# Reordering the setup of layer 0 in a four-layer graph network: first loads, degrees and weights

## The chip, the cores and the metric

The kernel runs on one core of one Trainium2 chip. Its time is the device time of one execution in microseconds; the median of several executions is given. The profile is of one further execution.

## What is computed

64 graphs of 256 nodes pass through four layers, each of the form "layer norm of x plus the layer's output". Layer 0 is a recurrence over the nodes; it is the only one that the change touches:

```
d         = sum(adj, axis=-1)                                # degree of each node
dinv      = where(d != 0, 1/d, 0)
norm_adjT = swapaxes(adj, 1, 2) * dinv[:, :, None]

def step(h, i):                                              # i = 0 .. 255, one after the other
    x     = h_e[:, i]
    x_par = einsum('bj,bjd->bd', norm_adjT[:, i], h)         # h: already updated up to i-1
    iou   = x @ W_ioux.T + b_ioux + x_par @ W_iouh.T + b_iouh
    r, z  = sigmoid(split(iou, 2))
    hc    = tanh(x @ W_coux.T + b_coux + (x_par * r) @ W_couh.T + b_couh)
    h[:, i] = z * x_par + (1 - z) * hc
```

Layers 1 to 3 (a graph convolution, a masked attention, an attention with 8 heads) come after it and are not changed.

## The kernel before

`_recurrence` computes layer 0. All 64 graphs go through a step together. Node i needs a sum over all nodes j of adj[j, i] times the state of j. For j not yet updated (j at or above i) that state is x itself, so this part is known from the start: it is the x side. The kernel computes the x side for columns i = 0 to 127 ahead of the steps, and that for columns 128 to 255 in gaps of the steps.

Four things happen ahead of step 0.

1. Setup (lines 124 to 164). `_load_wT` loads the four weight matrices on SP's queue (L48), transposes them on PE into PSUM (L52) and copies them to `WxT` and `WhT` on DVE (L53). Six bias loads go out on ACT's queue (L133, L137). DVE adds them and cuts the sum in three bf16 parts (`_split_bf16`, L60 to L67), each stored by SP into `bias3` (L68). POOL makes the identity `ident`, a pattern `span`, which SP copies to `window` in eight small DMAs (L153), zeroes `Hw` (L158) and makes the triangular mask `tri` (L161).

2. The x side for columns 0 to 127 (lines 185 to 209), in eight groups of GB = 8 graphs. A group loads two halves of adj (`xA`, 512 KB each, SP, L193) and of x (`xX`, 1 MB each, ACT, L194), POOL masks one half with `tri` (L195), PE makes two products for each graph, one for each half of the rows j (L172), ACT and DVE by turns copy PSUM to `xu` (L208), and SP stores it to `Us` in HBM (`x_out`, L179). Tiles have two buffers, so a group's loads wait for the products of the group before the last.

3. Tables of block 0 (the first 32 nodes). `degrees(0)` (lines 267 to 293) loads adj's rows in four parts of 4 rows into one buffer, `rows` (L276), and reduces each (L279), so that a part is loaded after the one before it is reduced; then it inverts the degrees, and four DMAs store them to `dinv` (L293). `load_S(0)` loads the 32 x 32 piece `S` of adj for each graph, in runs of 32 numbers, and doubles it over the partitions (L527, L534). `chain_S`, `late_load`, `sums_in` (`ACC` from `Us`, L298) and `load_x` (`xq`, L554) fill what step 0 and the steps after it read.

4. The start of step 0: `flip_x` transposes `xq` (L563), `x_part` and `bias_part` begin the gates in PSUM (L582, L573), `xp` is `ACC` times `dinv` (L685), and the step flips it (L597), multiplies by `WhT` (L590) and takes the Sigmoid (L779). In step 0, `flip_x` of the next eight nodes stands on PE ahead of that product and reads `xq_1`.

The pools for the x side are closed before those of the tables and the steps (`blk`, `stream`, `work`, `ps`) are opened, and the latter take their place in SBUF and PSUM. Up to the first step the tile framework chooses the order of the instructions on each engine and derives the waits. From `tc.manual_schedule()` (line 708) on, each engine runs in the order of the source. Each engine runs its own stream in order; SP and ACT also issue DMAs, and an engine stands still while it waits to issue one.

Of the kernel before, what the change touches and what calls it, by code (L numbers as in the profile page):

```python
# [9 lines left out]
F32 = mybir.dt.float32  # L10
BF16 = mybir.dt.bfloat16
AF = mybir.ActivationFunctionType
ALU = mybir.AluOpType
AX = mybir.AxisListType
# [5 lines left out]
P = 128  # L20
# [50 lines left out]
def _recurrence(tc, ident, Hd, x, adj, W_ioux, b_ioux, W_iouh, b_iouh, W_coux, b_coux, W_couh, b_couh):  # L71
# [22 lines left out]
    U = 8  # L94
# [8 lines left out]
    with ExitStack() as ctx:  # L103
# [13 lines left out]
        def ring(lo, hi):  # L117

            while lo < hi:
                end = min(hi, (lo // W + 1) * W)  # L120
                yield lo, end, lo % W
                lo = end

        with tc.tile_pool(name="r_setup", bufs=1) as tmp, tc.tile_pool(
            name="r_setup_ps", bufs=2, space=bass.MemoryType.PSUM
        ) as tps:
            for WT, wi, wc, s in ((WxT, W_ioux, W_coux, "x"), (WhT, W_iouh, W_couh, "h")):
                _load_wT(nc, tmp, tps, wi, ident, lambda c: WT[:, :, c % 2, c // 2 * 2, :], "i" + s)
                _load_wT(nc, tmp, tps, wc, ident, lambda c: WT[:, :, c, 1, :], "c" + s)
            bx, bh = (tmp.tile([1, 2, 3, P], F32, name=f"bias_{s}") for s in "xh")  # L130
            for t, bi, bc in ((bx, b_ioux, b_coux), (bh, b_iouh, b_couh)):
                for g in range(2):
                    nc.scalar.dma_start(  # L133
                        t[:, :, 2 * g, :],
                        bi[g * D:(g + 1) * D].rearrange("(c d) -> c d", c=2).unsqueeze(0),
                    )
                nc.scalar.dma_start(t[:, :, 1, :], bc.rearrange("(c d) -> c d", c=2).unsqueeze(0))  # L137
            nc.vector.tensor_add(bx, bx, bh)
            _split_bf16(nc, tmp, bias3, bx, "bias")

            span = tmp.tile([W, T // U, U], F32, name="span")
            nc.gpsimd.memset(span, 1.0)
            nc.gpsimd.affine_select(
                out=span, in_=span, pattern=[[U, T // U], [0, U]], compare_op=ALU.is_ge,
                fill=0.0, base=W - T // 2 - LAG - 1, channel_multiplier=-1,
            )
            for w in range(2):
                first = (w * T - W + T // 2) % W  # L150
                for lo, hi, at in ring(first, first + W):
                    for g in range(2):
                        nc.sync.dma_start(  # L153
                            window[w][g * W + at:g * W + at + hi - lo],
                            span[lo - first:hi - first].rearrange("p a u -> p (a u)"),
                        )
        nc.vector.memset(ones3, 1.0)
        nc.gpsimd.memset(Hw, 0.0)  # L158

# [16 lines left out]
        def x_out(half, b, ub):  # L176

            for c in range(2):
# [2 lines left out]
                    ub[:, :, c * P:(c + 1) * P],  # L181
                )


        with tc.tile_pool(name="r_first", bufs=2) as tmp, tc.tile_pool(
            name="r_first_ps", bufs=4, space=bass.MemoryType.PSUM
        ) as tps:
            for g in range(0, B, GB):
                A = tmp.tile([P, 2, GB, P], F32, tag="A", name=f"xA_{g}")
                Xs = tmp.tile([P, 2, GB, D], F32, tag="X", name=f"xX_{g}")  # L190
                for jc in range(2):
                    rows = slice(jc * P, (jc + 1) * P)
                    nc.sync.dma_start(A[:, jc], adj[g:g + GB, rows, 0:P].rearrange("b j i -> j b i"))  # L193
                    nc.scalar.dma_start(Xs[:, jc], x[g:g + GB, rows, :].rearrange("b j d -> j b d"))  # L194
                nc.gpsimd.tensor_mul(  # L195
                    A[:, 0], A[:, 0], tri.unsqueeze(1).to_broadcast([P, GB, P])
                )
                for n in range(0, GB, 4):
                    ub = tmp.tile([P, 4, D], F32, tag="ub", name=f"xu_{g}_{n}")
                    for e in range(0, 4, 2):  # L200
                        pb = tps.tile([P, 2, D], F32, tag="x", name=f"xp_{g}_{n}_{e}")
                        for q in range(2):
                            b = n + e + q
                            x_product(
                                pb, q, [A[:, jc, b, :] for jc in range(2)],
                                [Xs[:, jc, b, :] for jc in range(2)],
                            )
                        (nc.vector.tensor_copy if e else nc.scalar.copy)(ub[:, e:e + 2, :], pb)  # L208
                    x_out(0, g + n, ub)

        blk = ctx.enter_context(tc.tile_pool(name="r_blk", bufs=2))
        stream = ctx.enter_context(tc.tile_pool(name="r_stream", bufs=2))
        work = ctx.enter_context(tc.tile_pool(name="r_work", bufs=2))
        ps = ctx.enter_context(tc.tile_pool(name="r_ps", bufs=1, space=bass.MemoryType.PSUM))


        now = 0
# [49 lines left out]
        def degrees(k):  # L267

            R = 4
            HT = T // 2  # L270
            deg = work.tile([P, HT], F32, tag="deg", name=f"deg_{k}")
            for r in range(0, HT, R):
                rows = stream.tile([P, R, N], F32, tag="rows", name=f"rows_{k}_{r}", bufs=1)
                for h in range(2):
                    at = k * T + h * HT + r
                    nc.sync.dma_start(rows[h * B:(h + 1) * B], adj[:, at:at + R, :])  # L276
                yield
                for e in range(0, R, 2):
                    nc.vector.tensor_reduce(  # L279
                        deg[:, r + e:r + e + 2], rows[:, e:e + 2, :], AX.X, ALU.add  # L280
                    )
                    yield
            zero = work.tile([P, HT], F32, tag="deg0", name=f"deg0_{k}")
            nc.vector.tensor_scalar(zero, deg, 0.0, None, ALU.is_equal)
            nc.vector.tensor_add(deg, deg, zero)
            nc.vector.reciprocal(deg, deg)
            nc.vector.tensor_scalar(zero, zero, -1.0, 1.0, ALU.mult, ALU.add)
            nc.vector.tensor_mul(deg, deg, zero)
            yield
            for h in range(2):  # L290
                at = k * T + h * HT
                for c in range(2):
                    nc.sync.dma_start(dinv[c * B:(c + 1) * B, at:at + HT], deg[h * B:(h + 1) * B])  # L293

        def sums_in(a):

# [360 lines left out]
        pushes = []  # L657
        ring_in = []

        for _ in degrees(0):  # L660
            pass
        tables[0]["S"], double = load_S(0)
        double()
        tables[0]["Sd"] = chain_S(0)
        tables[0]["An"] = late_load(0)
        for a in range(3):
            sums_in(a)

        xq = {0: load_x(0)}
        for e in range(2):  # L670
            flip_x(0, e, xq[0])
            next_of(copies, 0)
        xq[1] = load_x(1)
        rc = ps.tile([P, 2, P], F32, tag="rc", name="rc_0", bufs=2)
        z = ps.tile([P, P], F32, tag="z", name="z_ps_0")
        for G, gates in ((rc, slice(0, 2)), (z, 2)):
# [695 lines left out]
```

## Time and profile before

| | |
|---|---|
| median of 3 runs | 3609.26 us (3601.38 to 3611.15) |
| profiled execution | 3613.04 us, span 3611.1 us |
| granted TensorE clock, mean | 0.975 |
| busy: PE, DVE, ACT, POOL | 91%, 66%, 53%, 41% of the span |
| from the span's start to the first load of the x side | 21.09 us |
| last store of the x side issued / landed | 120.93 / 123.45 us |
| `dinv` in place, first Sigmoid of step 0 | 151.9, 158.32 us |

Times in the profile count from the start of the span. A line such as `41.00 10.37 DMA Us<-xu` in the chain of waits says that from 41.00 us on, for 10.37 us, what ended last was waiting for that transfer. In busy time by stretch, each engine has its busy time in that stretch and the number of its instructions in brackets; "PEld" is the loading of PE's stationary operand, and the last three columns are the granted clock, the busy share of the DMA engines and what they moved.

### The profile page before, as it was taken

How to read it: one execution, taken by the hardware profiler on the slowest of the kernel's cores; microseconds unless marked ns; L12 is line 12 of the kernel's file. 1: busy time of each engine (PE TensorE's matmuls, PEld its weight loads, DVE VectorE, ACT ScalarE, POOL GpSimd, SP SyncE). 2: the span in 40 equal slices, each digit the busy share in tenths (PEclk: the TensorE clock that was granted, in tenths of full speed). 3: DMA queues.
4: the chain of work that ended last, by engine and by line, in shares of the span. 5: the costliest groups of instructions: out<-in, count | busy, mean ns of one | idle time of the engine just before them, and what ended most of it. 6: DMA issues, size and time to landing. Idle time of an engine off the chain costs nothing.

```text
span 3611.1 us, 81391 instructions
## 1 busy us (share of the span) xinstructions
PE 3296.8 (91%) x30374; PEld 2341.3 (65%) x30374; DVE 2375.3 (66%) x7052; ACT 1904.6 (53%) x5026; POOL 1485.1 (41%) x1669
## 2 busy tenths in 40 slices
PE   5599989999889898858999999999999999999998
PEld 4355555555555555536777777777777777777776
DVE  2366767776667777735676666677776667777775
ACT  0145545554445454425666666666666666666664
POOL 2266667766566778722222222222222222222221
PEclk9799999999999999978999999999999999999999
DMA  8746666788876564140111111111111111111100
GB/s 284 215 134 145 157 167 151 165 191 204 193 190 156 156 152 115 57 114 18 45 45 45 45 45 45 45 45 45 45 45 45 45 45 45 45 44 42 45 27 22
DMA packets 389636, 348.48 MB, mean 97 GB/s; under 512 B 107244, under 2 KB 355192, under 8 KB 384120
## 3 DMA queue, kind: packets, MB, share of 16 engines
q1 hardware_dynamic: 367280, 323.84, 33.7%
q10 hardware_dynamic: 21960, 19.41, 1.6%
q8 instruction: 242, 3.96, 0.5%
q14 instruction: 154, 1.26, 0.1%
HBM read 224.01 MB, written 99.61 MB: 90 GB/s over the span
## 4 chain that ended last, share of the span: by engine, by line
PE 71%; DVE 7%; DMA 7%; POOL 5%; issue 4%; ACT 4%; SPq 2%; ACTq 0%; DVEq 0%; POOLq 0%
PE mm L948 13%; PE o L1151 7%; PE rc L590 4%; PE s L1131 4%; PE rc L582 3%; PE mm_2f L948 3%; PE mm_3v L948 3%; PE mm_3f L948 3%; PE mm_g L948 3%; PE mm_t L948 3%; PE mm_2s L948 3%; PE mm_2v L948 3%; PE mm_2w L948 3%; DVE ACC L615 3%; PE tr_x L938 3%
## 5 line engine op out<-in xcount | busy, mean ns | idle before, releaser
L615 DVE SCALAR_TENSOR_TENSOR ACC<-keep,S,ACC 128x128 f32<-128x128 f32 x1712 | 504.1, 344 | 191.9 <-ACT hs L633 175.6
L917 POOL TENSOR_TENSOR rstd<-rstd,mhalf 128x2 f32<-128x2 f32 x256 | 172.9, 693 | 627.9 <-DVE rstd L916 626.2
L651 POOL TENSOR_TENSOR ACC<-ACC,far 128x384 f32<-128x384 f32 (+1 forms) x313 | 371.5, 1187 | 24.6
L1138 DVE TENSOR_TENSOR p<-s,neg 128x512 f32<-128x512 f32 x512 | 317.4, 681 | 69.0 <-PE s L1131 69.0
L582 PE MATMUL rc<-WxT,xqT 128*64 128x256 f32 x2048 | 328.9, 400 | 7.5 <-issue 2.5
L925 ACT ACTIVATE y<-y,shift,rstd 128x256 f32<-128x256 f32 x512 | 273.4, 598 | 92.4 <-DVE shift L923 53.0
L1043 POOL TENSOR_TENSOR y<-y,g 128x512 f32<-128x512 f32 x64 | 80.8, 1262 | 567.7 <-issue 556.8
L647 POOL TENSOR_TENSOR far<-hs,S 128x384 f32<-128x384 f32 (+1 forms) x313 | 304.2, 972 | 4.7
L1139 ACT ACTIVATE p<-p 128x512 f32<-128x512 f32 x512 | 294.8, 626 | 2.6 <-DVE p L1138 1.6
L913 DVE BATCH_NORM_STATS2 st<-y 128x6 f32<-128x256 f32 x512 | 208.9, 408 | 94.6 <-POOL y L1043 89.8
L755 POOL TENSOR_TENSOR ready<-ACC,dinv 128x128 f32<-128x128 f32 x255 | 101.9, 399 | 399.3 <-DVE ACC L615 380.2
L1166 DVE TENSOR_TENSOR y<-y,mm_3f 128x512 f32<-128x512 f32 x64 | 44.0, 687 | 281.3 <-PE mm_3f L948 281.3
L1157 DVE RECIPROCAL rT<-o 128x256 f32<-128x256 f32 x128 | 224.0, 1750 | 0.3 <-PE o L1151 0.3
L1054 ACT ACTIVATE qk<-mm,b_cols 128x256 f32<-128x256 f32 x256 | 107.2, 469 | 203.7 <-PE mm L948 203.7
L1029 ACT COPY xT<-tr_x 128x512 f32<-128x512 f32 x192 | 112.3, 586 | 183.0 <-PE tr_x L938 183.0
L599 ACT COPY xpT<-xpT_ps 128x128 f32<-128x128 f32 x256 | 68.1, 266 | 263.7 <-PE xpT_ps L597 263.7
L590 PE MATMUL rc<-WhT,xpT 128*64 128x128 f32 x2048 | 170.4, 288 | 28.7 <-ACT xpT L599 28.5
L590 PEld LDWEIGHTS rc<-WhT,xpT 128*64 128x64 f32 x2048 | 107.8, 137 | 118.5 <-ACT xpT L599 83.8
L948 PE MATMUL mm<-xT,W2q 128*128 128x256 f32 x512 | 129.4, 396 | 44.6 <-ACT xT L1029 44.6
L582 PE MATMUL z_ps<-WxT,xqT 128*64 128x128 f32 x2048 | 169.8, 287 | 0.0
L1106 ACT ACTIVATE qk<-mm,b_cols 128x256 f32<-128x256 f32 x256 | 107.2, 469 | 118.5 <-PE mm L948 118.5
L1008 POOL TENSOR_TENSOR dis<-dis,mhalf 128x2 f32<-128x2 f32 x64 | 44.1, 689 | 292.0 <-DVE dis L1007 292.0
(167 smaller groups left out, 7988.8 us busy)
## 6 DMA issues: line engine op xcount, KB each, us to landing
xX<-in_x_dram ACTq DMA_DIRECT2D x16, 1024.0 KB
Us<-xu SPq DMA_DIRECT2D x64, 256.0 KB
rows<-in_adj_dram SPq DMA_DIRECT2D x64, 256.0 KB
ACC<-Us SPq DMA_DIRECT2D x32, 512.0 KB
xq<-in_x_dram SPq DMA_DIRECT2D x64, 256.0 KB
Hw<-hs SPq DMA_DIRECT2D x512, 32.0 KB
Es<-eu SPq DMA_DIRECT2D x64, 256.0 KB
early_sb<-Es SPq DMA_DIRECT2D x32, 512.0 KB
```

The source lines that it names most:

```text
L582: nc.tensor.matmul(G[o * B:(o + 1) * B], xqT[a, i // 2][:, i % 2, kc, h * B:(h + 1) * B], WxT[:, kc, o, gates], start=False, stop=False, s ...
L590: nc.tensor.matmul(G[o * B:(o + 1) * B], hT[:, kc * B:(kc + 1) * B], WhT[:, kc, o, g], start=False, stop=(kc == 1), skip_group_check=True,)
L615: nc.vector.scalar_tensor_tensor(acc[:, 0, :], keep[:, j % 2, :], s, acc[:, 0, :], ALU.mult, ALU.add)
L647: nc.gpsimd.tensor_mul(tmp[:, 0:count, :], hs.unsqueeze(1).to_broadcast(shape), s.unsqueeze(2).to_broadcast(shape),)
L651: nc.gpsimd.tensor_add(acc, acc, tmp[:, 0:count, :])
L913: nc.vector.bn_stats(st, y[:, c, :])
L925: nc.scalar.activation(y[:, c, :], y[:, c, :], AF.Identity, bias=shift[:, c:c + 1], scale=rstd[:, c:c + 1],)
L948: nc.tensor.matmul(pm[:, c, :], lhsT[:, k, c * P:(c + 1) * P], rhs[:, k, :], start=(k == 0), stop=(k == 1),)
L1138: nc.vector.tensor_add(p, s_ps[i], self.neg3)
L1139: nc.scalar.activation(p, p, AF.Exp, scale=ISQ)
L1151: nc.tensor.matmul(o_ps[i * HD:(i + 1) * HD, part, :], ones if part else self.v3_sb[:, k, h * HD:(h + 1) * HD], self.ps_of[hc][i][:, k, :] ...
L1157: nc.vector.reciprocal(rT, o_ps[:, 1, :])
```

## The change

The first loads of the x side, for groups 0 and 8, are issued ahead of everything else, and behind them the 32 rows of adj for block 0's degrees in one tile, `rows_0`. `blk` is opened first, so `S` no longer takes the place of x-side tiles, and `load_S(0)` stands ahead of the x side. The loads of the later groups are issued after the products of the group two before them. The weights are loaded and transposed after the source's second group (g = GB), the degrees reduced, inverted and stored after its third; `dinv` is stored by the same four DMAs as before. `xq_1` is loaded right after `xq_0`, ahead of `ACC`. The steps are the same.

```diff
+        blk = ctx.enter_context(tc.tile_pool(name="r_blk", bufs=2))
+        stage = ctx.enter_context(ExitStack())
+        fst = stage.enter_context(tc.tile_pool(name="r_first", bufs=2))
+
+        def first_load(g):
+
+            A = fst.tile([P, 2, GB, P], F32, tag="A", name=f"xA_{g}")
+            Xs = fst.tile([P, 2, GB, D], F32, tag="X", name=f"xX_{g}")
+            for jc in range(2):
+                rows = slice(jc * P, (jc + 1) * P)
+                nc.sync.dma_start(A[:, jc], adj[g:g + GB, rows, 0:P].rearrange("b j i -> j b i"))
+                nc.scalar.dma_start(Xs[:, jc], x[g:g + GB, rows, :].rearrange("b j d -> j b d"))
+            return A, Xs
+
+        first_in = [first_load(g) for g in (0, GB)]
+
+        rows_0 = fst.tile([P, T // 2, N], F32, name="rows_0", bufs=1)
+        for h in range(2):
+            nc.sync.dma_start(rows_0[h * B:(h + 1) * B], adj[:, h * T // 2:(h + 1) * T // 2, :])
...
+        def weights():
             for WT, wi, wc, s in ((WxT, W_ioux, W_coux, "x"), (WhT, W_iouh, W_couh, "h")):
                 _load_wT(nc, tmp, tps, wi, ident, lambda c: WT[:, :, c % 2, c // 2 * 2, :], "i" + s)
                 _load_wT(nc, tmp, tps, wc, ident, lambda c: WT[:, :, c, 1, :], "c" + s)
...
-        for _ in degrees(0):
-            pass
         tables[0]["S"], double = load_S(0)
         double()
+
+
+        with tc.tile_pool(name="r_first_ps", bufs=4, space=bass.MemoryType.PSUM) as xps:
+            for g in range(0, B, GB):
+                A, Xs = first_in.pop(0)
+                nc.gpsimd.tensor_mul(
+                    A[:, 0], A[:, 0], tri.unsqueeze(1).to_broadcast([P, GB, P])
+                )
...
+                if g + 2 * GB < B:
+                    first_in.append(first_load(g + 2 * GB))
+                if g == GB:
+                    weights()
+                if g == 2 * GB:
+                    deg = fst.tile([P, T // 2], F32, name="deg_0", bufs=1)
+                    nc.vector.tensor_reduce(deg, rows_0, AX.X, ALU.add)
+                    inverse(deg, fst.tile([P, T // 2], F32, name="deg0_0", bufs=1))
+                    dinv_from(deg, 0)
+        stage.close()
+
+        stream = ctx.enter_context(tc.tile_pool(name="r_stream", bufs=2))
+        work = ctx.enter_context(tc.tile_pool(name="r_work", bufs=2))
+        ps = ctx.enter_context(tc.tile_pool(name="r_ps", bufs=1, space=bass.MemoryType.PSUM))
+
         tables[0]["Sd"] = chain_S(0)
         tables[0]["An"] = late_load(0)
+        xq = {a: load_x(a) for a in range(2)}
         for a in range(3):
             sums_in(a)
-
-        xq = {0: load_x(0)}
         for e in range(2):
             flip_x(0, e, xq[0])
             next_of(copies, 0)
-        xq[1] = load_x(1)
```

`inverse` and `dinv_from` are the arithmetic and the four stores that `degrees` had; `degrees` of the later blocks calls them.

## The prediction

> **What bounds the kernel now.** I read the page's span and slices first, then the chain of waits over the first 320 us, then busy time by stretch for the setup, then the order in time around the change. The chain over the setup (start us, us, what):
>
> ```profile
> 19.03 1.78 DMA window<-span
> 21.09 5.35 DMA xA<-in_adj_dram
> 26.70 2.35 POOL xA L195
> 29.09 9.49 PE xp L172 x32
> 41.00 10.37 DMA Us<-xu
> ...
> 120.93 2.52 DMA Us<-xu
> 124.33 4.33 DMA rows<-in_adj_dram
> 128.77 1.29 DVE deg L279 x2
> 130.62 4.18 DMA rows<-in_adj_dram
> 134.89 1.29 DVE deg L279 x2
> 136.72 3.98 DMA rows<-in_adj_dram
> 140.79 1.29 DVE deg L279 x2
> 142.61 4.61 DMA rows<-in_adj_dram
> 147.31 1.29 DVE deg L279 x2
> 152.03 3.62 DMA xq<-in_x_dram
> 157.02 1.28 ACT L779
> ```
>
> The reader is to see three serial pieces: a head (nothing of x or adj is asked for before 21.09 us), the x side (to 123.45 us, the last Us store landed), and a tail of four load-then-reduce rounds, after which step 0 begins (first Sigmoid at 158.32 us, behind the table load). Busy time by stretch says what limits each (stretch: length, then PE, PEld, DVE, ACT, POOL busy with counts; granted clock, DMA share, GB/s):
>
> ```profile
> 8.00:12.00 4.00, 1.11 (x4) 0.71 (x4) 3.79 (x7) 0.00 (x0) 1.82 (x4) 1.00 0.00 0
> 12.00:21.00 9.00, 5.58 (x20) 2.99 (x20) 6.87 (x15) 0.00 (x0) 0.00 (x0) 1.00 0.03 4
> 23.00:112.00 89.00, 61.70 (x229) 49.20 (x230) 9.68 (x14) 9.47 (x15) 18.78 (x8) 0.90 1.10 358
> 112.00:116.00 4.00, 4.00 (x12) 3.19 (x11) 0.00 (x0) 0.16 (x1) 0.00 (x0) 0.57 0.52 156
> 130.00:152.00 22.00, 2.38 (x12) 1.89 (x14) 4.80 (x13) 0.99 (x2) 2.85 (x5) 0.50 0.69 191
> ```
>
> From 8 to 21 us the DMA engines carry nothing. From 23 to 112 us they are full: 358 GB/s at a share above 1, PE 61.7 of 89 us. So the x side is bound by bytes (33.62 MB between 21 and 124 us by the DMA view), not by a compute engine, and the tail by latency.
>
> **The change, part by part.** The instruction streams of the two kernels are the same on every engine from step 0 to the end, so all of the effect lies ahead of the first Sigmoid. Two facts of the new streams depart from the source's order: the degree reduction of block 0 stands on DVE ahead of the first PSUM copy of group 0, and SP has windows, bias parts and S ahead of group 0's stores. Also, in both kernels a DMA waits for the one issued eight before it.
>
> 1. First loads. They go out at about 0.8 us (where the weight loads are now) in place of 21.09: minus 20.3 us. Work displaced by that: ident, span, Hw and tri on POOL end at 9.9 us, so group 0's mask starts then and not at 6.4; four 512 KB and four 1 MB loads are asked for meanwhile, so the DMA engines do not notice.
>
> 2. Bytes moved into the x side. rows_0 is 2.10 MB, the weights 1.57, S and its copy 0.52: 4.19 MB by 358 GB/s is 11.7 us. S goes in runs of 128 bytes; the two us in which it goes today (128 to 130) show 126 GB/s at full share, so its 0.26 MB takes 2.1 us and not 0.7: plus 1.4. Sum 13.1 us (11.7 to 15).
>
> 3. Tail. Out go 123.45 to 158.32, 34.9 us. In comes, after the last store: four xq issues and one ACC issue at 0.59 us each (3.0); the 1.57 MB of these, from 2.0 us on, at 250 GB/s (this stage shows 191 and 204) land by about 8.3; then xp 1.41 (L685), transpose and copy 0.7, h_part 0.66, table load 1.28. That is 12.4 us (9 to 16), as stream tiles take the place of the first pool's and every xq load waits for all its stores. xq_1 is now ahead of ACC, so the 3.62 us that flip_x(1, 0) of step 0 waits today goes. Gain 22.5.
>
> 4. Weights within groups 16 and 24. 24 transposes, 6.7 us of PE, and 12 copies of 0.43 us on DVE go among products that fill 8 of each 11.6 us group; their 1.5 MB queue on SP behind A of group 24. PE stands at the first transpose, in front of group 16's last product, until nat_ix lands; X of group 32 waits for that product. Two groups in flight cover it (0 to 3 us, within step 6). If the cover is gone, it costs those 3 us.
>
> 5. Bias chain, dinv stores, Sd. Six ACT bias loads now stand behind X, seven DVE operations (5 us) end near 35 us and are needed at 117; the four dinv stores take 2.4 us of SP once, when SP has 4 of 11.6 us in use; seven DVE reductions less. Nothing: the transfers of the x side hide them. Uncovered, the dinv stores would cost 2.4 us.
>
> 6. The queue at the start. The first 8.4 MB (two groups and rows_0) land by 0.8 + 2 + 8.4/0.358 = 26 us. The reduction waits for rows_0, then takes 8 x 0.68 = 5.5 us at most (4.3 if the fixed part of one falls away). Behind it on DVE: a bias cast, the copy of group 0 that its first store waits for; behind that store on SP: the S copy, a bias part, three stores, A of group 16. So stores start at about 33 and A of group 16 at 36. On ACT, X of group 16 waits for the second half of rows_0 (eight back). Between 26 and 36 the engines could carry 3.6 MB, and X of group 16, S, group 0's stores and the beginning of A are about as much, but late in it. No row shows this. From below: nothing, if X fills it. From above: the whole 10 us. I take 4, by the 2 to 3 us between one store round and the next load that this stage shows already.
>
> Here a rule speaks against the change. The row: eight window DMAs, each issued after an earlier one landed or not, take SP 4.97 us, 0.62 each. The Trainium skill, "DMA: Bandwidth & Descriptors", section "Anatomy of one DMA", gives every DMA about 2.0 us of setup and completion (fitted on another issuing path). Eleven small DMAs stand on SP between the landing of rows_0 and A of group 16. By the row they take 6.8 us, beside the reduction; by the rule, were each to wait for its completion, 22 us, and the gain would fall by 15. I go by the row, since most wait for bias loads that have long landed.
>
> Another concerns the clock. The stretch from 130 to 152 us was granted 0.50, that from 152 to 159 0.91. The same skill, "TensorE: Matmul & The Clock Gate", Part 1, lets the clock halve after one idle window of about 3.4 us. A tail of 12 us idles for longer than that, so step 0 starts on a slow clock as now: no gain. Were the gap short enough, the 4.07 us of PE in that last stretch would win 0.4. No difference in the sum.
>
> **Sum.** 20.3 + 22.5 - 13.1 - 4 = 25.7 us. The profiled execution took 3613.04 us (span 3611.1), 3.8 above the median of the three runs, 3609.26; a difference carries over, so 3609.3 - 25.7 = 3583.6, about 3584 us. With all bounds the gain is 14 (13.1 at 15, tail at 16, start at 10) to 35 (11.7, 9 and 0), 3574 to 3595; the three runs spread by 10, so some 5 us on either side come on top.
>
> **The rivals.**
> - SP's queue at the start holds stores and loads back for longer (the skill's 2 us each, or X of group 16 waiting for rows_0, windows and S in turn): a hole of 10 to 20 us. For: SP is in order, and eight in flight is soon full of small ones. Against: 0.62 us by the row. Against the 4 us taken that costs 6 to 16 more: 3590 to 3600 (by the rule 3599: gain 25.7 - 15.2).
> - The start goes better: no hole, xq and ACC land fast, gain 33 to 37, about 3574. For: 372 GB/s in the first full stretches of the x side. Against: DVE waits first for rows_0.
> - The change does not do what it says: the load order makes the same bytes arrive, and the x side plus start-up end no earlier, since step 0 waits for something else. Then within 3 us of 3609. Against: the chain names nothing else between 124 and 152 us than rows, deg and dinv.
> - Slower: the PE clock in the recurrence. The 28 us rest ahead of it (clock 0.50) shrinks to 10. If the throttle keeps account of load over a longer time, the 1400 us of the steps run at a lower grant; PE is busy 1270 of them. For: the grant varies already, as here:
>
> ```profile
> 157.00:357.00 200.00, 180.32 (x2199) 108.48 (x2197) 136.22 (x471) 99.57 (x343) 126.82 (x148) 0.99 0.56 142
> 957.00:1157.00 200.00, 176.84 (x2228) 102.05 (x2226) 129.14 (x438) 91.51 (x319) 127.43 (x140) 0.93 0.74 175
> ```
>
>   Against: the dip comes 800 us after the rest. It costs 1270 x d/0.98 for a drop d, so it outweighs 25.7 us from d = 0.02; at 0.03 the time is 3609 - 26 + 39 = 3622.
>
> **How the numbers follow.** Forecast (gain 20 to 32) 0.66; held start 0.17; better start 0.11; no effect 0.03; lower clock 0.03. About 0.3%, 10.8 us, is what a measurement of this kernel can tell from no change. Faster by more: 0.66 + 0.11 + the four fifths of the held start that lie below 3598, 0.90 in all. Slower: the clock, 0.03. Same: the rest, 0.07. The range 3568 to 3600 takes in the bounds with 5 us of run spread, and leaves out some of the held start and the last two cases.
>
> **What would show it.** Right: xA and xX issues at about 1 us; 340 GB/s or more from 3 us to about 107 with one dip between 26 and 37; one reduction over 128x4096 of 4.3 to 5.5 us ending near 31; last Us store landed near 120; dinv nowhere in the chain; first Sigmoid near 132. Wrong: GB/s below 200 for over 10 us after 26 us; PE waiting on nat_ix for more than 4 us while DMA falls; the last store past 128; or recurrence steps of a different length (1400 us of them at a clock other than 0.98).

## The result and the profile after

| | before | after |
|---|---|---|
| median | 3609.26 us (3601.38 to 3612.8, 5 runs) | 3594.13 us (3587.5 to 3596.16, 5 runs) |
| ratio of after to before | | 0.9958, 95% interval 0.9942 to 0.9974 |
| span of the profiled execution, clock | 3611.1 us, 0.975 | 3592.7 us, 0.974 |
| first load of the x side | 21.09 us | 0.80 us |
| last store of the x side landed | 123.45 us | 127.93 us |
| first Sigmoid of step 0 | 158.32 us | 140.83 us |
| first Sigmoid to the end | 3452.8 us | 3451.9 us |

The kernel is faster, by 15.1 us in the medians, where 25.7 were forecast. Between the two profiled executions nearly the whole difference lies ahead of the first Sigmoid: it comes 17.5 us earlier, and what follows it has the same length within 0.9 us.

The chain of waits over the setup of the kernel after (start us, us, what):

```profile
7.21 17.42 DMA rows<-in_adj_dram
24.65 6.39 DMA bias_h<-in_L_gnn_b_couh_dram
31.16 0.96 DVE bias_x L162
...
34.84 4.33 DVE deg L688
39.16 0.47 DVE bias L63
39.63 0.60 DVE xu L680
...
41.63 7.05 DMA Us<-xu
...
61.02 6.84 DMA nat_ix<-in_L_gnn_W_ioux_dram
...
125.41 2.52 DMA Us<-xu
...
130.69 6.85 DMA ACC<-Us
137.56 0.45 DVE xp L716
...
139.53 1.28 ACT L810
```

The head of before is gone, and so are the four rounds of rows and deg at its end: between the last Us store and the table load there is one ACC load. In their place the chain has a new piece at the start. It goes from rows to a bias load, to the bias arithmetic, to the degree reduction, and only then to the first copy on DVE and the first store of the x side. The forecast had the reduction in this place; it had the bias chain in the shade of the transfers.

Busy time by stretch of the kernel after (PE, PEld, DVE, ACT, POOL; then clock, DMA share, GB/s) shows what that costs:

```profile
4.00:20.00 16.00, 8.57 (x31) 7.14 (x32) 0.00 (x0) 0.00 (x0) 9.58 (x8) 1.00 1.15 375
20.00:24.00 4.00, 0.49 (x3) 0.09 (x1) 0.00 (x0) 0.00 (x0) 0.00 (x0) 1.00 0.98 213
24.00:28.00 4.00, 0.78 (x2) 0.50 (x2) 0.00 (x0) 2.36 (x3) 0.00 (x0) 0.69 0.99 209
28.00:32.00 4.00, 2.22 (x5) 1.51 (x5) 0.84 (x1) 0.00 (x0) 0.00 (x0) 0.50 0.30 59
32.00:36.00 4.00, 4.00 (x11) 3.03 (x9) 3.86 (x6) 0.00 (x0) 0.00 (x0) 0.53 0.02 2
36.00:40.00 4.00, 0.22 (x2) 0.00 (x0) 4.00 (x3) 0.00 (x0) 0.00 (x0) 0.90 0.73 231
40.00:44.00 4.00, 3.71 (x9) 3.00 (x10) 3.28 (x10) 0.00 (x0) 0.00 (x0) 0.50 0.99 195
...
52.00:104.00 52.00, 36.30 (x152) 28.82 (x152) 10.23 (x21) 4.68 (x8) 9.37 (x4) 0.86 1.10 355
```

The DMA engines are full up to 20 us and again from 44 us on. Between, six stretches move 909 x 4 us = 3.64 MB where 358 GB/s would have moved 8.59: 4.96 MB are missing, 13.8 us' worth. This number, "the gap" from here on, is taken in the same way from 20 to 44 us for every kernel below. Two things are to be told apart in it. From 20 to 28 us the engines are busy (share 0.98) but move only 211 GB/s: these are the rows (from 20 to 24 us SP's queue, on which nothing else is left, carries 0.79 of 0.85 MB). From 28 to 36 us the engines move next to nothing (59 and 2 GB/s), and DVE goes through bias parts and the reduction; X of group 16 is issued at 35.67 us.

### The profile page after: what moved, and what is told of

Its sections match the earlier page's. It is cut to its first block, busy times and chain, and to the rows that moved or that the text cites. A ratio compares the mean times of both kernels' runs of the same rounds, so it can differ in the third digit from the quotient of the medians.

```text
span 3592.7 us, 81338 instructions
## 1 busy us (share of the span) xinstructions
PE 3299.4 (92%) x30374; PEld 2342.2 (65%) x30374; DVE 2373.0 (66%) x7045; ACT 1905.7 (53%) x5026; POOL 1486.9 (41%) x1669
## 4 chain that ended last, share of the span: by engine, by line
PE 72%; DMA 7%; DVE 6%; POOL 5%; issue 4%; ACT 3%; SPq 2%; ACTq 0%; DVEq 0%; POOLq 0%
PE mm L979 13%; PE o L1182 7%; PE rc L590 4%; PE s L1162 4%; PE mm_3v L979 3%; PE mm_2f L979 3%; PE rc L582 3%; PE mm_3f L979 3%; PE mm_t L979 3%; PE mm_g L979 3%; PE late L506 3%; PE mm_2w L979 3%; PE mm_2s L979 3%; PE mm_2v L979 3%; PE tr_x L969 3%
## 5 line engine op out<-in xcount | busy, mean ns | idle before, releaser
L196 PE MATMUL xp<-xX,xA 128*128 128x256 f32 x384 | 114.7, 437 | 64.8 <-POOL xA L667 32.3
```

## The experiments

Each kernel is the changed kernel with the edit shown, unless the text names another one under it; "..." in an edit marks lines left out. Medians were taken in three series, each beside the kernel before, whose medians were 3607.93, 3607.65 and 3607.55 us. The changed kernel was measured for the result above and again in the third series, not in the first two, so kernels of different series are compared by their ratios. By the intervals spread_all and degrees_after stand apart from both measurements of the changed kernel, acc_first_spread just touches one of them, and the others overlap; for those the argument rests on the order of events in the traces. The first Sigmoid is from one profiled execution each; the changed kernel, profiled twice, had it at 140.83 and 142.69 us, so 2 us of it are chance.

| kernel | median us | ratio to before (95%) | gap us | last Us landed us | first Sigmoid us |
|---|---|---|---|---|---|
| changed kernel | 3594.13 | 0.9958 (0.9942 to 0.9974) | 13.8 | 127.93 | 140.83 |
| bias_first | 3585.34 | 0.9944 (0.9927 to 0.9960) | 5.2 | 127.22 | 140.94 |
| reduce_pinned | 3594.28 | 0.9960 (0.9943 to 0.9976) | 13.1 | 135.04 | 147.84 |
| win_pinned | 3591.01 | 0.9961 (0.9944 to 0.9977) | 9.7 | 129.72 | 142.44 |
| rows_spread | 3586.32 | 0.9935 (0.9915 to 0.9954) | 9.7 | 126.06 | 139.22 |
| bias_moved | 3580.51 | 0.9927 (0.9905 to 0.9948) | 8.4 | 124.35 | 137.45 |
| bias_moved_spread | 3582.31 | 0.9929 (0.9906 to 0.9951) | 3.9 | 119.24 | 132.20 |
| degrees_after | 3603.00 | 0.9985 (0.9977 to 0.9993) | 9.1 | 119.43 | 153.43 |
| xq_early | 3593.15 | 0.9954 (0.9939 to 0.9969) | 13.9 | 137.15 | 145.24 |
| weights_early | 3590.90 | 0.9951 (0.9939 to 0.9963) | 10.9 | 131.93 | 144.78 |
| spread_all | 3574.72 | 0.9910 (0.9897 to 0.9923) | 3.6 | 121.97 | 134.16 |
| acc_first_spread | 3576.83 | 0.9927 (0.9912 to 0.9941) | 3.5 | 121.49 | 134.46 |
| changed kernel again | 3587.65 | 0.9955 (0.9941 to 0.9968) | 14.2 | 129.76 | 142.69 |

### First series: which link holds the gap open

**bias_first**: the bias loads and their arithmetic ahead of the first loads.

```diff
+        bx, bh = (tmp.tile([1, 2, 3, P], F32, name=f"bias_{s}") for s in "xh")
...
+        _split_bf16(nc, tmp, bias3, bx, "bias")
         first_in = [first_load(g) for g in (0, GB)]
```

> The six bias loads go ahead of the first x loads on ACT's queue, everything else as in the changed kernel, in which the DMA engines miss 13.8 us worth of bytes between 20 and 44 us, the last bias load lands at 31.0 and the first Sigmoid comes at 140.8. Theory (the late bias loads hold DVE, through DVE the bias store on SP, and through SP the next group's x loads): the hole shrinks to about 5 us, first Sigmoid near 132, time near 3585. Rival 1 (SP's small DMAs themselves cost about 2 us each): no change, Sigmoid 139 to 142. Rival 2 (it is the degree reduction ahead of the copies): it stays ahead of the second copy, so only some 3 us come back.

Measured: the reduction starts at 29.88 us in place of 34.77, and the gap falls to 5.2 us. But the six small loads now stand before X on ACT, whose first X load goes out at 5.03 us in place of 0.80, and the three bias stores hold SP from 9.69 to 18.54 us, ahead of the second half of the rows. So the x side starts slowly, and the first Sigmoid is where it was. Busy time by stretch of bias_first, against 375 GB/s in the first 16 us of the kernel after:

```profile
4.00:20.00 16.00, 1.22 (x2) 0.50 (x2) 10.31 (x9) 1.28 (x1) 11.31 (x8) 1.00 1.06 289
20.00:44.00 24.00, 15.74 (x62) 12.76 (x62) 7.12 (x9) 1.76 (x3) 0.00 (x0) 0.97 1.08 281
```

The 86 GB/s lost for 16 us are 3.8 us. The edit closes one gap by opening another; of the bias chain alone it says little. That its median meets the 3585 us of the theory is chance: the theory had the first Sigmoid near 132 us. The time came from behind it, where this execution took 3438.2 us and the changed kernel's two took 3451.9 and 3440.7.

**reduce_pinned**: the reduction stays where the source has it, behind the copies of groups 0, 8 and 16 on DVE.

```diff
-                    nc.vector.tensor_reduce(deg, rows_0, AX.X, ALU.add)
+                    tc.keep_in_program_order(
+                        nc.vector.tensor_reduce(deg, rows_0, AX.X, ALU.add)
+                    )
```

> The degree reduction of block 0 is held on DVE behind the copies of group 16, where the source has it. Theory (late bias loads): DVE is free for group 0's copies 4.4 us earlier, but SP and the x loads still wait for the bias chain; 1 to 2 us, Sigmoid 139 to 140. Rival 2 (the reduction is the cause): 4.4 us or more, Sigmoid at or below 136. Rival 1 (small DMAs): nothing.

Measured, on DVE and on SP in this kernel:

```profile
38.11 0.55 DVE L63 CAST bias<-bias_rest 1x768 bf16<-1x768 f32 x1
...
40.35 5.07 SPq L68 DMA_DIRECT2D bias<-bias  x1
45.52 1.08 SPq L203 DMA_DIRECT2D Us<-xu  x2
```

Group 0's copy on DVE starts at 35.96 us, 3.6 us earlier than in the kernel after. The first store does not follow it: it is issued at 45.52 us, because the last bias part stands ahead of it on SP for 5.07 us. Its DVE operation was over at 38.66; what else it waits for the trace does not name (X of group 16, issued on ACT from 36.96 us on, was on its way). The first Sigmoid comes at 147.84, 7 us later, where 139 to 140 was expected. The reduction is therefore not what the store waits for once it is moved; the next link takes over.

**win_pinned**: the eight window DMAs behind group 8's stores on SP.

```diff
+        def windows():
...
+                        tc.keep_in_program_order(nc.sync.dma_start(window[w][...], span[...]))
...
                 if g == GB:
                     weights()
+                    windows()
```

> The eight window DMAs go out behind group 8's stores on SP; DVE's and ACT's orders stay. Theory (late bias loads, and the x loads of group 16 held by the DMA eight before them, a window): x of group 16 goes out near 28 us and not at 35.7, the stores of group 0 still at 40 to 41; 3 to 5 us come back, Sigmoid 136 to 138. Rival 1 (2 us for each small DMA on SP): up to 13 us come back, Sigmoid near 128, time near 3582. Rival 2 (reduction): nothing.

Measured: X of group 16 leaves 4.6 us earlier (31.09 in place of 35.67 us), the first store at 40.82 in place of 41.06. The gap is 4 us smaller, but the end of the x side is not earlier, and the first Sigmoid is at 142.44, where the theory had 136 to 138 and the rival of the small DMAs 128. Seven windows take 4.38 us of SP in the kernel after and lie beside the DVE chain: taking them away moves the store by 0.2 us.

**rows_spread**: rows_0 on every other partition.

```diff
-            nc.sync.dma_start(rows_0[h * B:(h + 1) * B], adj[:, h * T // 2:(h + 1) * T // 2, :])
+            nc.sync.dma_start(rows_0[h::2], adj[:, h * T // 2:(h + 1) * T // 2, :])
...
-                    dinv_from(deg, 0)
+                    dinv_from(deg, 0, lambda h: slice(h, P, 2))
```

> Each half of the 32 rows goes to every other partition (0, 2, .. and 1, 3, ..) and not to 64 neighbouring ones; bytes and result stay. Between 20 and 28 us the changed kernel moves 211 GB/s at a DMA share of 0.98. If transfers into 64 neighbouring partitions are what is slow, this stretch rises above 330 GB/s, the bias loads behind it land some 3 us earlier and the Sigmoid comes at about 138. If it is slow for another reason (few queued transfers, long rows), the stretch stays at 211 and the Sigmoid at 140 to 141.

Measured, busy time by stretch of this kernel:

```profile
12.00:20.00 8.00, 8.00 (x30) 6.40 (x29) 0.00 (x0) 0.00 (x0) 2.35 (x1) 1.00 1.14 402
20.00:24.00 4.00, 0.74 (x4) 0.31 (x2) 0.00 (x0) 1.45 (x2) 0.00 (x0) 1.00 0.93 389
24.00:28.00 4.00, 3.48 (x10) 2.61 (x11) 1.60 (x3) 0.90 (x2) 0.00 (x0) 0.72 0.15 50
```

The same bytes that moved at 211 GB/s and a full share into 64 neighbouring partitions move at 389 into every other one. The bias sum starts at 26.33 us in place of 31.16, the first store at 36.09. The first Sigmoid is 1.6 us earlier than in the first profile of the changed kernel and 3.5 earlier than in the second. Against the first, most of the 4.1 us that the gap lost were lost again behind it, so this step alone is within the chance of one profile.

### Second series: the chain taken apart

**bias_moved**: the six bias loads, the sum and the split stay behind group 24's first work; each load and the sum stand within `tc.keep_in_program_order`. Unlike bias_first, this puts nothing before X.

```diff
                 if g == GB:
                     weights()
+                if g == 3 * GB:
+                    biases()
```

> Like the changed kernel, but the six bias loads, the sum and the three-part split are held back until group 24's work is on the engines; nothing else is edited. Theory (the bias chain holds the hole open: its last load lands at 31.04 us and DVE's chain up to 34.8 stands ahead of the degree reduction): the reduction starts near 30 us, when rows_0 has landed, and ends near 34.5; the first Us store goes out near 36 in place of 41.06; the GB/s missing between 20 and 44 us shrink from 13.8 us' worth to about 9; the first Sigmoid comes at about 136 (140.83 in the changed kernel), the time 3589. Rival (the hole is set by SP's chain of small DMAs and the wait for eight back, the bias chain only stands in its shade): the reduction starts early, but the first Us store still goes out at 39 to 41, the first Sigmoid stays within 1.5 us of 140.8.

Measured, DVE in order of time in this kernel (start us, us):

```profile
0.86 0.11 DVE L185 MEMSET ones<- 3x64 bf16 x1 [0.86 <-PEq L1394]
30.34 4.42 DVE L694 TENSOR_REDUCE deg<-rows 128x16 f32<-128x4096 f32 x1 [29.37 <-DMA rows<-in_adj_dram]
34.68 1.28 DVE L684 COPY xu<-xp 128x512 f32<-128x512 f32 x2
```

and in the kernel after:

```profile
31.16 0.95 DVE L162 TENSOR_TENSOR bias_x<-bias_x,bias_h 1x768 f32<-1x768 f32 x1 [30.18 <-DMA bias_h<-in_L_gnn_b_couh_dram]
32.14 0.55 DVE L60 COPY bias_rest<-bias_x 1x768 f32<-1x768 f32 x1
...
34.77 4.40 DVE L688 TENSOR_REDUCE deg<-rows 128x16 f32<-128x4096 f32 x1
```

The bracket is what the engine was idle for: in bias_moved DVE goes from the memset straight to the reduction and waits for the rows alone. It is done 4.4 us earlier, group 0's copies follow at once, and the first store is issued at 35.43 us in place of 41.06. Gap 8.4 us (about 9 expected), first Sigmoid 137.45 (about 136 expected). The theory holds: the bias chain was on the path. Of the 5.6 us that the store gained, 4.4 are the earlier reduction; the rest is not taken apart. For without the bias loads and stores the framework also orders the queues otherwise: the windows go out from 12.34 us on in place of 30.23, and X of group 16 at 30.83 in place of 35.67. So it is win_pinned that rules out the rival, SP's chain of small DMAs: there too the windows and X of group 16 had moved, but not the bias chain, and the store stayed at 40.82.

**bias_moved_spread**: both edits together.

> The run before it, and rows_0 laid over every other partition instead of 64 neighbouring ones. Theory (the hole is the sum of the slow rows_0 transfer, the bias chain and the reduction): rows_0 complete near 25 us, the reduction from there to 29.5, the first Us store near 31, the missing GB/s between 20 and 44 us down to about 4 us' worth; at 52 us about 15.4 MB moved (12.7 in the changed kernel). If the x side hands all of it on, the first Sigmoid comes at about 132 and the time is 3585. Rival (what is won at the start is lost again at the end of the x side, as in the run with rows_0 spread alone, because the last group's products then run behind a pause of PE): the first Sigmoid between 136 and 139.

Measured, busy time by stretch:

```profile
20.00:24.00 4.00, 1.52 (x8) 0.99 (x6) 0.00 (x0) 0.00 (x0) 0.00 (x0) 1.00 0.94 390
24.00:28.00 4.00, 1.97 (x5) 1.60 (x6) 2.84 (x1) 0.00 (x0) 0.00 (x0) 0.77 0.38 108
28.00:32.00 4.00, 4.00 (x17) 3.34 (x16) 3.49 (x8) 0.00 (x0) 0.00 (x0) 0.80 1.07 371
32.00:36.00 4.00, 2.46 (x12) 1.82 (x10) 0.00 (x0) 0.00 (x0) 0.00 (x0) 1.00 1.20 317
36.00:40.00 4.00, 0.00 (x0) 0.00 (x0) 0.69 (x1) 0.58 (x1) 0.00 (x0) 0.98 1.03 257
40.00:44.00 4.00, 0.00 (x0) 0.00 (x0) 0.69 (x1) 0.58 (x1) 0.00 (x0) 0.50 1.11 359
```

One low stretch is left, 24 to 28 us, in which the rows have landed and DVE reduces (2.84 of 4 us). The reduction starts at 25.16 us, the first store goes out at 30.24. The gap is 3.9 us, and here the x side hands it on: the last store lands at 119.24 us, the first Sigmoid is at 132.20. This is the setup that was forecast for the changed kernel (a gap of 4 us, last store near 120, Sigmoid near 132), and the median lies 25.3 us below that of the kernel before, against 25.7 forecast. In the medians it is not told apart from bias_moved (3582.31 and 3580.51), although its first Sigmoid is 5.3 us earlier.

**degrees_after**: one part of the change undone; the degrees are computed after the x side again, in four rounds. The framework then also moves the weights' loads to the front (nat_ix is issued at 11.99 us in place of 61.02).

```diff
-        rows_0 = fst.tile([P, T // 2, N], F32, name="rows_0", bufs=1)
...
+        for _ in degrees(0):
+            pass
         tables[0]["Sd"] = chain_S(0)
```

> The first loads, S and the weights as in the changed kernel, but block 0's degrees as before the change: after the x side, in four rounds of load and reduce; no rows_0. The weights then stand further ahead, next to the first groups. Theory (the degree rounds in the tail cost about 22 us, rows_0 and the reduction at the start cost 5.9 us of bytes and most of the hole of 13.8 us): the last Us store lands at 112 to 118 us (127.9 in the changed kernel), the tail is 30 to 35 us, the first Sigmoid at 144 to 152, the time 3597 to 3604: most of what is won at the end was paid for at the start, and the degrees are worth 3 to 10 us. Rival (the hole at the start is not made by rows_0 and its reduction): the last store lands only 6 us earlier, near 122, the first Sigmoid near 155, the time 3608.

Measured: last store 119.43 us, tail 34.0 us, first Sigmoid 153.43 us, median 3603.0 (3597 to 3604 expected). The Sigmoid and the last store are both 1.4 us later than the ranges given for them. Against 140.83 and 142.69 us of the changed kernel the degrees' part, with the other place of the weights, is worth 11 to 13 us where 3 to 10 were expected, so most of the gain of the whole change. And the gap is still 9.1 us without any rows: the bias sum starts at 28.54 us, and group 0's copy on DVE comes behind five operations of the bias chain, at 32.14. The first loads without the degrees' part bring 0.0015 of the time (interval 0.0007 to 0.0023). What fills its tail, from the chain of waits:

```profile
116.93 2.50 DMA Us<-xu
...
120.15 4.27 DMA rows<-in_adj_dram
...
124.69 1.29 DVE deg L283 x2
...
126.51 4.05 DMA rows<-in_adj_dram
...
```

**xq_early**: xq_0 and xq_1 in the pool that is open from the start, loaded among the last groups.

```diff
-            xq = stream.tile([P, U // 2, D], F32, tag="xq", name=f"xq_{a}")
+            xq = blk.tile([P, U // 2, D], F32, tag="xq", name=f"xq_{a}")
...
+                if g == B - 3 * GB:
+                    xq = {a: load_x(a) for a in range(2)}
...
-        xq = {a: load_x(a) for a in range(2)}
```

> Like the changed kernel, but xq_0 and xq_1 live in the pool that is open from the start and are loaded among the loads of the last groups. Theory (the tail from the last Us store to the first Sigmoid, 12.9 us, is four xq issues, then ACC): ACC is issued first after the last store lands and shares the DMA engines only with the other ACC tiles: it lands some 5 us earlier, the table load and the Sigmoid follow; tail 8 to 9.5 us. The 1.05 MB of xq come into the x side: plus 3 us (64 neighbouring partitions: up to 5). Net 0 to 2 us gained, first Sigmoid 139 to 141. Rival (xq is not what the tail waits for): tail 12 to 13 us, first Sigmoid 143 to 146, slower than the changed kernel by 3 to 5 us.

Measured: the tail falls from 12.9 us to 8.1 (137.15 to 145.24), as the theory has it. But the x side ends 9.2 us later than in the first profile of the changed kernel (7.4 against the second), not 3 to 5. SP stands 3.6 and 3.2 us at two of the xq issues, in front of stores and of A. The first Sigmoid is 4.4 us later (2.6 against the second). The median, 3593.15, does not show it: the changed kernel's own two medians, 3594.13 and 3587.65, lie further apart.

### Third series: what is left

**spread_all**: bias_moved_spread with xq on every other partition as well.

```diff
-                nc.sync.dma_start(xq[h * B:(h + 1) * B], x[:, at:at + U // 2, :])
+                nc.sync.dma_start(xq[h::2], x[:, at:at + U // 2, :])
...
-                    G[o * B:(o + 1) * B], xqT[a, i // 2][:, i % 2, kc, h * B:(h + 1) * B],
+                    G[o * B:(o + 1) * B], xqT[a, i // 2][:, i % 2, kc, h::2],
```

> The run with the bias chain held back and rows_0 on every other partition, and xq laid over every other partition too. Theory (a transfer into 64 neighbouring partitions is slow because of where it lands): the 1.05 MB of xq between the last Us store and ACC, which moved at 200 to 250 GB/s, move at 350 to 430; the tail from the last Us store landed (119.2 us) to the first Sigmoid, 13.0 us, falls to 10.5 to 11.5; the first Sigmoid at 129.5 to 131, the time 3579. Rival (the tail is set by the number of issues and the fixed time of a DMA, not by the rate): tail 12.5 to 13, first Sigmoid 132.

Measured: tail 12.2 us (13.0 in bias_moved_spread; 10.5 to 11.5 expected), first Sigmoid 134.16 (129.5 to 131 expected), so the theory of the tail is mostly refuted. The transfers did not get as fast as it had them: from 124 to 128 us the engines moved 279 and 244 GB/s, not 350 to 430. The chain of waits of this kernel shows what came next:

```profile
123.47 3.35 DMA xq<-in_x_dram
126.83 1.93 PE xqT_ps L567 x8
128.75 1.91 PE rc L586 x8
130.66 0.83 PE z_ps L586 x8
...
132.86 1.28 ACT L816
```

With xq earlier, PE is the next to be late: 6.0 us of transposes and products stand between the landing of xq and the table load, where in the changed kernel ACC's landing at 137.54 us was the last.

Yet this is the fastest kernel of all: 3574.72 us, 12.9 below the changed kernel on the same chip, and the two intervals are apart. Of that, 8.5 us are the earlier first Sigmoid (134.16 against 142.69). The rest is not explained. The clock was higher in these runs (0.978 to 0.979 in all five, 0.973 to 0.978 in the six of the changed kernel), and a gain of the steps from the other layout of xq is not seen: from the first Sigmoid to the end this execution took 3441.5 us, the second of the changed kernel 3440.7.

**acc_first_spread**: spread_all with ACC_0 issued ahead of xq.

```diff
+        sums_in(0)
         xq = {a: load_x(a) for a in range(2)}
-        for a in range(3):
+        for a in range(1, 3):
             sums_in(a)
```

> The run before it, with ACC_0 issued ahead of xq_0 and xq_1. Theory (the tail is bound by the bytes that step 0 needs, and they are the same in either order): the first Sigmoid within 1 us of the run before it, at 129.5 to 131.5. Rival (ACC_0 is the last to land only because it stands behind xq): ACC_0 lands 2 to 3 us earlier, the first Sigmoid at 127.5 to 129.

Measured: first Sigmoid 134.46 us, tail 13.0. ACC_0 does land early, 3.9 us after the last store (9.6 in bias_moved_spread), but xq lands at 127.8 us in place of 126.8, and step 0 waits for it and for the same work on PE. So the order of these loads makes no difference to the first Sigmoid, as the theory had it; the rival falls.

**weights_early**: another part undone; the weights next to the first groups.

```diff
+        weights()
         bx, bh = (tmp.tile([1, 2, 3, P], F32, name=f"bias_{s}") for s in "xh")
...
-                if g == GB:
-                    weights()
```

> The changed kernel with one part undone: the weights are loaded and transposed next to the first groups, behind rows_0 on SP, and not behind the second group. Theory (the missing GB/s between 20 and 44 us are 13.8 us' worth because nothing else stands in the queues; the weights' 1.57 MB would move in that gap and no longer among groups 16 and 24): by 44 us some 1.5 MB more have moved than in the changed kernel (10.12 MB), the last Us store lands at about 123.5 (127.9), the first Sigmoid at 136 to 137, the time 3590. Rival (the gap is held open by what DVE has to do ahead of the first copies, and the weights' twelve PSUM copies of 0.43 us come on top of it there): the first Us store goes out 2 to 5 us later than 41.06, what the gap gains is lost, the first Sigmoid at 140 to 142.

Measured: by 44 us 0.96 MB more have moved, so part of the gap is filled. But the first store goes out at 47.38 us, 6.3 later than in the changed kernel, and the first Sigmoid is at 144.78. The rival's mechanism held, and its price was low by 3 us. Behind the reduction ten copies of the weights, and bias parts between them, stand on DVE ahead of group 0's copy, which starts at 45.59 us in place of 39.56:

```profile
39.88 0.73 DVE L53 COPY WxT<-wt_ix 128x256 f32<-128x256 f32 x2
...
44.92 0.76 DVE L53 COPY WhT<-wt_ih 128x256 f32<-128x256 f32 x2
45.59 0.68 DVE L681 COPY xu<-xp 128x512 f32<-128x512 f32 x1
```

In the medians, 3590.9 against 3587.65, the two can't be told apart. So filling the gap with bytes is not enough; what stands behind the gap has to move.

**after_again**: no edit.

> The changed kernel itself, once more, beside the three kernels above it. First Sigmoid at 140 to 142 us. If the forecast's missing 10 us lie in the setup alone, its median is 8 to 12 us above that of the kernel with both holes closed; if part of it is the clock of the steps, whose granted share went from 0.973 to 0.979 between executions, the distance goes up to 16.

Measured: 3587.65 us with the first Sigmoid at 142.69, and 12.9 us above spread_all. The first of the two theories gave 8 to 12 and the second up to 16; the first Sigmoids account for 8.5 of it. How much one kernel varies behind the first Sigmoid is seen between its two profiles: 3451.9 us to the end in the execution with a mean clock of 0.974, 3440.7 us in that with 0.977. Busy time from the first Sigmoid to the end of the steps, first and second profile:

```profile
140.83:1558.40 1417.57, 1289.97 (x16454) 762.73 (x16456) 974.93 (x3340) 697.44 (x2438) 962.40 (x1065) 0.98 0.62 153
...
142.69:1548.10 1405.41, 1278.21 (x16454) 756.64 (x16456) 974.69 (x3340) 698.06 (x2438) 963.33 (x1066) 0.99 0.62 155
```

The whole difference lies in the steps (1417.6 and 1405.4 us; the layers behind them took 2034.3 and 2035.3). PE was busy 11.8 us less for the same 16454 products, at a granted clock of 0.99 in place of 0.98, and the other three engines were busy within 1 us of the same time.

## Why the prediction was right, and where its sum was not

The prediction was faster at 3584 us with a range to 3600; 3594.13 lies in it, and the changed kernel's second median, 3587.65, too. The direction and the three large terms were right for the reasons given; the term for the start was not, and the gain came out 10.6 us smaller than its sum. That the range held is in part luck: the case that reaches from 3590 to 3600 was put there for two reasons that were not the ones. By its steps:

1. **First loads, 20.3 us.** Right. They go out at 0.80 us; group 0's mask starts at 9.04 (9.9 forecast), and the engines move 375 GB/s from 4 to 20 us.
2. **Bytes into the x side, 13.1 us.** Right as far as it can be seen: the long full stretch runs at 355 GB/s (358 before).
3. **Tail, 34.9 to 12.4 us.** Right: 12.9 us, though two parts of it were off in opposite ways: ACC landed 9.6 us after the last store (8.3 forecast), and what follows took 3.3 us (4.05), since `xp` took 0.44 us and not 1.41.
4. **Weights, 0 to 3 us.** Right. `nat_ix` landed at 67.86 us, late in the chain, but PE waited only 0.8 us for it, and the engines kept 345 to 371 GB/s from 52 to 68 us. Loading them at the start instead (weights_early) did not help.
5. **Bias chain, dinv stores, Sd at nothing, since the transfers hide them.** Wrong for the bias chain; right for the rest. The dinv stores took 5.24 us of SP (2.4 forecast) at 75.46, without a place in the chain. The bias chain was costed by when its result is needed (117 us). It should have been costed by where it stands: on DVE ahead of the reduction and of group 0's copy, for which the first store, and behind it on SP the next loads, wait. Its last load, behind X and five others on ACT, was issued at 24.65 us, when the chain of waits shows a rows transfer landing, and took 6.39 us more to land. The chain has nine DVE operations of 6.1 us, not seven of 5; five of them, 3.6 us, stood ahead of the reduction. bias_moved puts a number on it: gap 13.8 to 8.4 us, first Sigmoid 3.4 us earlier than the first profile of the changed kernel and 5.2 earlier than the second.
6. **The queue at the start, 4 us of at most 10.** The mechanism was named (rows, reduction, copy, store, A) and the size was wrong: 13.8 us, above the upper bound. The reduction took 4.40 us (4.3 to 5.5 forecast) but ended at 39.17 and not near 31. The forecast had the stores start at about 33; they started at 41.06. Two terms were missing under it. One is the bias chain. The other is the rate: "8.4/0.358" took rows_0 at the full 358 GB/s, and the rows moved at 211 and were there at 30.3 us, not 26 (seen in bias_moved, where the reduction waits for them alone). bias_moved and rows_spread together remove both, and the gap becomes 3.9 us: the number of the sum, for a kernel without these two terms. That it comes so near is partly chance, since the 4 us were chosen between 0 and 10 and not summed.

The terms add up: the x side from its first load to its last store took 127.1 us in place of 102.4, so 24.8 longer where 13.1 + 4 were forecast (7.7 too much), and the tail 0.5 more. The gap is 9.8 us above its 4, so some 2 us came back elsewhere on the x side; 0.8 of them are the first 16 us at 375 GB/s in place of 358. 25.7 - 8.2 is the 17.5 us by which the first Sigmoid moved. What follows it gave 0.9 us. The medians give less, 15.1, because the profiled execution before lay 3.8 us above its median and that after only 0.4 above its own; the forecast let the 3.8 carry over.

Of the signs that it named, the first loads, the single reduction of 4.40 us and the absence of dinv from the chain came true. The reduction near 31, the last store near 120 and the first Sigmoid near 132 did not, and one sign of being wrong did: below 200 GB/s for 12 us in all after 26 us (three stretches of 4 us with 59, 2 and 195). The last store, at 127.93 us, stayed just inside its limit of 128; in the second profile, at 129.76, it did not.

**The rivals.** The time fell where the held start had it, a case given 0.17: a gap of 10 to 20 us and 3590 to 3600 us. The likeliest case, a gain of 20 to 32, is missed by the first medians (15.1) and, by 0.1, by the second (3607.55 - 3587.65 = 19.9). But the two reasons given for the held start were not the ones. Small DMAs at 2 us each on SP (the figure of the Trainium skill, "DMA: Bandwidth & Descriptors", section "Anatomy of one DMA", given there for another issuing path) would have cost 22 us; seven windows took 4.38 us, 0.63 each, and moving them away (win_pinned) brought the first store forward by 0.2 us. X of group 16 did wait for the windows, but with the windows moved (4.6 us earlier X) the end of the x side stayed. That the change does nothing is out by the intervals. The slower clock in the steps did not come: from the first Sigmoid on, 3451.9 us against 3452.8 between the first profiles, and 3440.7 in the second.

The prediction also weighed a clock rule, without effect on the sum. The trace agrees with the weighing: the stretch from 128 to 136 us was granted 0.50, as before in the longer tail, although this tail is only 12.9 us.

## What to carry to other kernels

A small operation that is needed late is not free because its result is needed late. Ask where it stands in the queue of its engine, what input it waits for there, and who stands behind it. Here a small load that landed late and 3.6 us of arithmetic on one partition held the first store of the x side, and holding it back helped while moving it to the front did not. And when a large transfer is added to a sum at the rate of the stage, look at where it lands: the rate of other tiles is not its rate.

## What was unexpected in the hardware

- **Neighbouring partitions.** rows_0, 2 x 1 MB into 64 neighbouring partitions each, moved at 209 to 213 GB/s at a DMA share of 0.98 to 0.99. Into every other partition, the same rows from the same addresses moved at 389 to 399 GB/s at 0.93 to 0.95 (20 to 24 us of four kernels). The Trainium skill, "SBUF — State Buffer", section "Door 1: The DMA port swizzle", has a rule that fits and that the prediction did not draw on: a transfer reaches only the ports of its own partitions, and 64 neighbouring ones reach 8 of 16. No run here shows the ports themselves. 2.10 MB at 211 and not 358 GB/s are 9.9 us in place of 5.9, which puts the landing of the rows at 30 us in place of 26, where it was seen (30.3). The same page, section "Can I just issue two DMAs to hit both halves?", says that only one transfer over all 128 partitions reaches every port; here 64 partitions in steps of two moved at no lower rate than 128 did (375 GB/s from 4 to 20 us), and the measurement decides. That the share reads full at both rates means that a full share does not show the bytes at their peak.
- **The clock of the steps is a matter of the execution.** The same kernel took 3585.17 us at a mean clock of 0.977 and 3598.12 us at 0.973, and its two profiles differ by 12.2 us in the steps alone. Kernels that run the same steps took between 1404.8 and 1418.7 us for them. With gains of 10 us, the order of events ahead of the first Sigmoid separates kernels that the medians do not, as long as they differ by more than its own 2 us. What sets the clock of an execution no run here shows.
